# Products woven into two attention streams, early norms, pools handed over tile by tile, and a later quantised product in a twelve-stage Perceiver kernel

## The chip, the cores and the metric

The kernel runs on one core of a Trainium2 chip. A core has five engines that run side by side, each through its instructions in order: TensorE (PE in the profile, its weight loads PEld), VectorE (DVE), ScalarE (ACT), GpSimd (POOL) and SyncE (SP), which here only issues DMAs. The metric is the device time of the whole program in microseconds (us); the median of three runs stands for a kernel.

## The reference

x has 16 sequences of 64 tokens with 256 features; a context has 16 sequences of 1601 rows. Twelve blocks follow each other, and each adds to x what it computes from the layer norm of x:

```python
x = x + L0_xattn(norm(x), ctx)      # softmax attention over the context, 16 heads
x = x + L0_attn(norm(x))            # sqrt(D)*x + position, 4 layers of linear attention + relu MLP, last norm
x = x + L0_ffn(norm(x))             # 8 experts, capacity, gelu
x = x + L1_xattn(norm(x), ctx)      # slot attention: 3 iterations with a GRU
x = x + L1_attn(norm(x))            # softmax attention among 64 tokens, bias, own input
x = x + L1_ffn(norm(x))             # router, 8 experts, 2 integration steps, refinement
x = x + L2_xattn(norm(x), ctx, mask)# relu(scores)^2 attention over the context
x = x + L2_attn(norm(x))            # attention by relu features
x = x + L2_ffn(norm(x))             # 16 experts, 8 of them chosen, and a shared one
x = x + L3_xattn(norm(x), ctx)      # softmax attention over the context
x = x + L3_attn(norm(x))            # causal softmax attention, relative bias
h = norm(x)                         # L3_ffn: rows rounded to 8 bits
s = max(abs(h), axis=-1) / 127
x = x + (clip(round(h / s), -128, 127) @ Wq.T) * s * weight_scale + bias
```

Here norm subtracts the mean of a row and divides by its standard deviation.

## The kernel before, in words

The 1024 tokens are NT = 8 tiles of 128 rows; x stays in SBUF as [128, 8, 256]. A product over 256 features is KC = 2 matmuls, into which the operand goes transposed, so that a stage starts as: statistics of each tile on VectorE (bn_stats, bn_aggr), a square root on ScalarE (rstd, L125), the normalised rows xln on VectorE, transposes on TensorE (tr), evictions, first product.

Each block is a method that opens pools of its own: sb and sb2 (SBUF, one and two buffers) and ps (PSUM). The list STAGES calls them in order; the last two blocks share l3_attn. Weights come through one pool that lives for the whole program (w2 with eight buffers, w8 with three). A pool is released at the end of its stage, and its bytes go to the stage behind. By default a tile on bytes of released pools waits for every user of those pools.

The order on an engine is partly written. keep_in_program_order pins an instruction behind the one that was traced before it on its engine; what is not pinned is ordered by a scheduler when the program is built. self.mm and self.tr (L2196, L2202) pin TensorE's instructions while self.pinned is set, and the class Written (L50) pins whatever VectorE, ScalarE or GpSimd get through it; linear attention uses it for all three (V, A, G).

Stage by stage, where the change reaches:

- l0_xattn and l2_xattn run through stream (L2091). It walks over pairs of context chunks of 128 rows: 16 sequences of NCH = 13 chunks are 208 chunks and 104 turns, and 9 turns more ahead of them. In turn k it issues the scores of turn k + 1 (weights), the projections of keys and values 18 chunks ahead (project, PSUM tag "bk"), and the weighted sums of chunks 2k and 2k + 1 (values, tag "acc"); a sequence is finished four chunks after its end (finish, which divides by the sums and fills hT). The last nine turns have no projections. Behind the stream self.lin makes the output product of all eight tiles, and add_to_x (L345) adds each to x.
- l0_attn works on two halves of x, a and b, of four tiles each. A half has its own buffers (class Half). measure takes statistics of a pair of tiles, norm normalises a pair, turn transposes a pair and evicts it to hT. project, attend and feed are generators that yield after each step; go(it, n) lets one run n steps, and mix lets the attention of one half run with the MLP (feed) of the other. begin makes the two norms at the start (of x, then of sqrt(D) x + position). The squares of the context for a later stage are taken on ScalarE in between, from pieces that come over ScalarE's DMA queue.
- l3_attn calls token_attention, whose loop at L2354 has ten turns. Turn t makes the scores of tile t, the values of tile t - 1 and the output product of tile t - 2. An object then adds the quantised block: prepare (L1989) takes one or two finished tiles, norms them, finds the largest value, scales, rounds by adding a large number, clamps (L2011) and writes f_xq; turn (L2017) transposes f_xq into f_qT; product multiplies, adds and stores a tile. In each turn one ready tile gets turn and product.

## Time and profile before

| what | us |
|---|---|
| median of three runs (3853.12 to 3859.05) | 3857.69 |
| profiled execution | 3857.84 |
| its span, first to last instruction | 3856.1 |
| TensorE busy | 3540.6 |
| VectorE busy | 1996.7 |
| ScalarE busy | 1455.9 |
| GpSimd busy | 1258.6 |

The span's 40 slices show TensorE's busy share and its granted clock, in tenths:

```
PE   8999999987999899999987998999999789999985
PEclk9999999998999889999989999999999979999987
```

Where the stages lie on the span, by the first transposes or products of each: l0_xattn to 865, l0_attn to 1331, l0_ffn to 1477, l1_xattn to 1999, l1_attn to 2090, l1_ffn to 2416, l2_xattn to 3080, l2_attn to 3196, l2_ffn to 3559, l3_xattn to 3713, the last layer to the end at 3856.

How to read the profile's lines. A timeline line is: start, duration, engine, line of the source, operation, output<-inputs, shapes, type, count, and in brackets how long the engine stood ahead of it and whose result ended that. A waits line is: who waited for whom, total, times, longest. A line of the chain that ended last is: start, duration, what ran. Helpers record under their own line: L2203 is tr, L2198 is mm, L58 is Written, L191 is lin. The granted clock is TensorE's, as a share of its full rate.

### The profile page before, as it was taken

To read this page: it belongs to the slowest core of one execution; us is meant where nothing else is said; L and a number is where in the kernel's file an instruction comes from. 1 tells how busy PE (TensorE), PEld (TensorE's weight loads), DVE (VectorE), ACT (ScalarE), POOL (GpSimd) and SP (SyncE) were. 2 spreads that over 40 slices of the span, in tenths; PEclk is the share of its full clock that TensorE was granted. 3 is DMA by queue.
4 is the path that set the end of the run, shared out by engine and by line. 5 is a ranking of instruction groups with operands and counts; after the bars stand their busy time and mean duration, and the time that the engine had idled before them with its cause. 6 is when DMAs were issued, how large, how long until landed. Compare 5 with 4: busy or idle time off the path is not lost.

```text
span 3856.1 us, 71175 instructions
## 1 busy us (share of the span) xinstructions
PE 3540.6 (92%) x31178; PEld 2237.7 (58%) x31178; DVE 1996.7 (52%) x3673; ACT 1455.9 (38%) x2067; POOL 1258.6 (33%) x749
## 2 busy tenths in 40 slices
PE   8999999987999899999987998999999789999985
PEld 4555555553566555555545666676767555555554
DVE  4333333335555435556556644577767655333346
ACT  2333333333444302444423434366666612111222
POOL 1555555551110002334331100477777530000011
PEclk9999999998999889999989999999999979999987
DMA  3111110001333214422301000311111004111730
GB/s 123 37 37 37 37 37 34 22 26 53 93 98 94 77 30 170 142 84 95 107 26 38 1 6 1 108 37 55 37 55 37 11 1 170 39 39 29 297 149 13
DMA packets 99678, 248.86 MB, mean 65 GB/s; under 512 B 8180, under 2 KB 69247, under 8 KB 97192
## 3 DMA queue, kind: packets, MB, share of 16 engines
q1 hardware_dynamic: 92456, 217.05, 15.9%
q10 hardware_dynamic: 6912, 27.27, 2.3%
q8 instruction: 245, 4.01, 0.4%
q14 instruction: 65, 0.53, 0.0%
HBM read 243.24 MB, written 1.05 MB: 63 GB/s over the span
## 4 chain that ended last, share of the span: by engine, by line
PE 77%; DVE 12%; ACT 7%; issue 2%; DMA 1%; POOL 0%; ACTq 0%; SPq 0%; DVEq 0%; POOLq 0%
PE sc L2198 15%; PE pk L2198 15%; PE lin L2198 6%; PE acc L2198 6%; PE lin L191 5%; PE lin_t L2198 5%; ACT e L319 5%; PE pu L2198 3%; PE gate L1770 3%; PE up L1770 3%; PE pc L1397 3%; PE prz L2198 2%; PE lin_t L178 2%; PE gelu_t L1307 2%; PE turn L2203 2%
## 5 line engine op out<-in xcount | busy, mean ns | idle before, releaser
L2134 POOL TENSOR_TENSOR tot<-tot,e 128x1024 f32<-128x1024 f32 (+1 forms) x340 | 803.4, 2363 | 375.0 <-ACT e L319 252.0
L262 DVE TENSOR_REDUCE m<-sc 128x4 f32<-128x2048 f32 x96 | 220.1, 2293 | 273.3 <-PE sc L2198 272.2
L1537 DVE SCALAR_TENSOR_TENSOR e<-sc,row_L_xattn_nbias,free 128x2048 f32<-128x2048 f32 x104 | 244.3, 2349 | 124.4 <-PE sc L2198 118.8
L1539 ACT ACTIVATE e<-e 128x2048 f32<-128x2048 f32 x104 | 198.8, 1912 | 242.8 <-DVE e L1537 242.8
L319 ACT ACTIVATE e<-sc 128x2048 f32<-128x2048 f32 x104 | 195.3, 1877 | 241.4 <-PE sc L2198 233.8
L2198 PE MATMUL sc<-qb,kT 32*128 32x128 f32 x6656 | 247.0, 285 | 39.3 <-DVE m L276 12.3
L2198 PEld LDWEIGHTS sc<-qb,kT 32*128 32x128 f32 x6656 | 208.1, 188 | 84.6 <-issue 25.1
L2198 PE MATMUL acc<-e,v 128*32 128x128 f32 x6656 | 228.4, 278 | 6.8 <-ACT e L1540 6.8
L2198 PEld LDWEIGHTS acc<-e,v 128*32 128x32 f32 x6656 | 171.3, 110 | 105.6 <-issue 95.0
L2198 PE MATMUL pk<-cT,wk 128*128 128x512 f32 (+1 forms) x512 | 207.6, 534 | 3.6 <-DVE rows L292 3.6
L2198 PE MATMUL pk<-wv,cT 128*128 128x256 f32 x832 | 208.6, 392 | 0.0
L1540 ACT ACTIVATE e<-e 128x2048 f32<-128x2048 f32 x104 | 198.9, 1912 | 3.3
L2198 PE MATMUL pk<-cT,wkv 128*128 128x512 f32 (+1 forms) x512 | 196.3, 524 | 0.0
L2198 PE MATMUL pk<-wkv,cT 128*128 128x256 f32 x832 | 196.3, 386 | 0.0
L2198 PEld LDWEIGHTS pk<-wv,cT 128*128 128x128 f32 x832 | 149.1, 189 | 75.3 <-issue 57.2
L2198 PEld LDWEIGHTS pk<-wkv,cT 128*128 128x128 f32 x832 | 153.2, 190 | 28.5 <-issue 4.3
L1397 PE MATMUL pc<-ew,eh 128*128 128x256 f32 x640 | 156.7, 387 | 0.0
L1774 ACT ACTIVATE g<-gate 128x512 f32<-128x512 f32 x68 | 40.7, 599 | 293.2 <-PE gate L1770 293.2
L942 POOL TENSOR_TENSOR e<-e,mx 128x512 f32<-128x512 f32 x96 | 81.7, 883 | 212.7 <-DVE mx L941 212.7
L2198 PE MATMUL sc<-kT,qb 32*128 32x512 f32 (+2 forms) x1536 | 139.5, 462 | 12.2 <-ACT e L319 0.7
L2198 PE MATMUL pu<-cn,e 128*64 128x257 f32 (+1 forms) x1248 | 143.7, 387 | 5.6 <-POOL e L952 5.6
L2198 PE MATMUL sc<-cT,qT 128*64 128x512 f32 (+1 forms) x768 | 142.2, 519 | 0.9 <-DVE qT L900 0.5
(488 smaller groups left out, 6392.4 us busy)
## 6 DMA issues: line engine op xcount, KB each, us to landing
cT<-in_ctx_t SPq DMA_DIRECT2D x128, 832.0 KB
cn<-in_ctx_n SPq DMA_DIRECT2D x32, 1664.0 KB
piece<-in_ctx_n ACTq DMA_DIRECT2D x32, 640.0 KB
w<-in_L_attn_W SPq DMA_DIRECT2D x8, 1024.0 KB
piece<-in_ctx_n ACTq DMA_DIRECT2D x16, 384.0 KB
w<-in_L_ffn_W SPq DMA_DIRECT2D x16, 256.0 KB
down<-in_L_ffn_w_down SPq DMA_DIRECT2D x16, 256.0 KB
gate<-in_L_ffn_w_gate SPq DMA_DIRECT2D x16, 256.0 KB
```

Source lines behind the costliest of these rows:

```text
L178: nc.tensor.matmul(pm, w[:, k, n * P : (n + 1) * P], xT[:, k, h * 512 : (h + 1) * 512], start=(k == 0), stop=(k == kc - 1),)
L191: nc.tensor.matmul(pm, xT[:, k, t * P : (t + 1) * P], w[:, k, :], start=(k == 0), stop=(k == kc - 1))
L262: nc.vector.tensor_reduce(x.m4[:, g, :, i], pm, AX.X, ALU.max)
L319: nc.scalar.activation(e, pm, AF.Exp, scale=0.25)
L942: pin(nc.gpsimd.tensor_tensor(p.e, p.e, p.mx.unsqueeze(2).to_broadcast(p.shape), ALU.subtract))
L1397: nc.tensor.matmul(pc[:, n, j, :], s.eh[i][:, c, tok], ew2[:, c, cols], start=False, stop=(c == 3))
L1537: nc.vector.scalar_tensor_tensor(e16, pm16, nb, free[:, at : at + P].unsqueeze(1).to_broadcast([P, 16, P]), ALU.add, ALU.mult)
L1539: nc.scalar.activation(e, e, AF.Relu)
L1540: nc.scalar.activation(e, e, AF.Square)
L1770: nc.tensor.matmul(pm[-1], w[:, k, n * P : (n + 1) * P], xT[:, k, tok], start=(k == 0), stop=(k == KC - 1))
L2134: nc.gpsimd.tensor_tensor(tot[:w], x.first if c == 1 else tot[:w], e[:w], ALU.add)
L2198: ins = self.nc.tensor.matmul(*args, **kw)
```

## The change

- **Output products in the streams.** stream gets a function out(t), which makes the product of tile t and adds it to x, with a PSUM tile of the projections' tag. Turns k = 96 to 102 call it for tiles 0 to 6 behind the scores of the next turn and ahead of the sums; tile 7 comes after the last finish. The call of self.lin goes.
- **Linear attention's start.** begin becomes start(s, p) for one pair. For half a (both pairs) and b (first pair) statistics, start and norm are traced before the projection of a, with VectorE's part not pinned; ScalarE's part stays pinned. The second pair of b is traced between steps of project(a). GpSimd's addition of the last norm's bias to x is moved behind project(a). Half makes its tiles in a written order, PSUM of attention has a pool of its own (ps_kv), and small statistics tiles move from sb2 to sb.
- **Linear attention's loop.** In feed, measure(y, 1) is a step of its own behind the last product; the loop runs it with one more go(fd, 1), behind the first step of project.
- **Pools.** All stage pools get reuse_waits="tile": a tile waits only for users of earlier tiles on its own bytes (in PSUM, its own bank). The pools of l0_attn, l1_xattn, l1_ffn, l2_attn and l3_xattn get side="right", which lays them from the other end of SBUF.
- **Last layer.** The norm of prepare is one small VectorE instruction and two ScalarE activations per tile in place of one VectorE instruction; the clamp is on GpSimd for tiles 0 to 5. The loop takes tiles that were prepared two or more turns before, all at once; behind the loop turn and product alternate.

```diff
@@ -51,11 +51,13 @@
     def __init__(self, tc, engine):
-        self.tc, self.engine = tc, engine
+        self.tc, self.engine, self.pinned = tc, engine, True
...
         def issue(*args, **kw):
-            self.tc.keep_in_program_order(getattr(self.engine, name)(*args, **kw))
+            ins = getattr(self.engine, name)(*args, **kw)
+            if self.pinned:
+                self.tc.keep_in_program_order(ins)
         return issue
...
@@ -325,8 +327,13 @@
-            self.stream(ps, sb2, load, wk, wv, copy, weights, finish, extra)
-            self.lin(ps, wo, hT, self.add_to_x, tag="acc")
+            def out(t):
+                pm = ps.tile([P, D], F32, tag="bk", name="lin", padded_shape=[P, 512])
+                for k in range(KC):
+                    self.mm(pm, hT[:, k, t * P : (t + 1) * P], wo[:, k, :], start=(k == 0), stop=(k == KC - 1))
+                self.add_to_x(t, pm)
+
+            self.stream(ps, sb2, load, wk, wv, copy, weights, finish, out, extra)
...
@@ -422,20 +430,22 @@
                     s.x = self.x[:, i * HT : (i + 1) * HT, :]
-                    for name, shape in (
-                        ("y", [P, HT, D]), ("n", [P, HT, D]), ("tmp", [P, HT, D]), ("kz", [P, HT, D]),
-                        ("va", [P, HT, 2, 136]), ("hT", [P, KC, 512]), ("qT", [P, KC, 512]), ("h1T", [P, 8, 512]),
-                    ):
-                        setattr(s, name, sb.tile(shape, F32, tag=f"{name}{i}", name=name))
+
+                shapes = dict(y=[P, HT, D], n=[P, HT, D], tmp=[P, HT, D], kz=[P, HT, D], va=[P, HT, 2, 136],
+                              hT=[P, KC, 512], qT=[P, KC, 512], h1T=[P, 8, 512])
+
+                def make(s, *names):
+                    for name in names:
+                        setattr(s, name, sb.tile(s.shapes[name], F32, tag=f"{name}{s.i}", name=name))
...
-                mv = sb2.tile([P, 2, 2], F32, tag=f"ln_mv{s.i}", name="ln_mv")
+                mv = sb.tile([P, 2, 2], F32, tag=f"ln_mv{s.i}", name="ln_mv", bufs=2)
                 for j in range(2):
-                    st = sb2.tile([P, 6], F32, tag="ln_st", name="ln_st", bufs=3)
+                    st = sb.tile([P, 6], F32, tag="ln_st", name="ln_st", bufs=3)
                     V.bn_stats(st, src[:, 2 * p + j, :])
                     V.bn_aggr(mv[:, j, :], st)
-                r = sb2.tile([P, 2], F32, tag=f"ln_r{s.i}", name="ln_r")
+                r = sb.tile([P, 2], F32, tag=f"ln_r{s.i}", name="ln_r", bufs=2)
                 V.tensor_scalar(r, mv[:, :, 1], 1.0, 1e-5, ALU.mult, ALU.add)
@@ -549,7 +559,7 @@
-                    pk = ps.tile([P, 2, 512], F32, tag="kv", name="pk")
+                    pk = ps_kv.tile([P, 2, 512], F32, tag="kv", name="pk")
                     for g in range(2):
@@ -620,11 +630,13 @@
                     V.tensor_tensor(s.y[:, t, :], pm, s.y[:, t, :], ALU.add)
-                    if t % 2:
-                        measure(s, s.y, t // 2)
-                    elif t:
+                    if t == 1:
+                        measure(s, s.y, 0)
+                    elif t == 2:
                         finish(s, 0, last)
                     yield
+                measure(s, s.y, 1)
+                yield
                 finish(s, 1, last)
@@ -640,27 +652,17 @@
-            def begin(s):
-
-                measure(s, s.x, 0)
-                yield
-                measure(s, s.x, 1)
-                yield
-                for p in range(2):
-                    mv, r = s.by[p]
-                    less = sb2.tile([P, 2], F32, tag=f"less{s.i}", name="less")
-                    V.tensor_scalar(less, mv[:, :, 0], -1.0, 0.0, ALU.mult, ALU.add)
-                    V.reciprocal(r, r)
-                    V.tensor_scalar(r, r, math.sqrt(D), 0.0, ALU.mult, ALU.add)
-                    for j in range(2):
-                        t = 2 * p + j
-                        A.activation(s.n[:, t, :], s.x[:, t, :], AF.Identity, bias=less[:, j : j + 1])
-                        V.scalar_tensor_tensor(s.y[:, t, :], s.n[:, t, :], r[:, j : j + 1], pos, ALU.mult, ALU.add)
-                    measure(s, s.y, p)
-                    yield
-                    norm(s, s.y, p)
-                    yield
-                G.tensor_tensor(s.x, s.x, lnf[:, D:].unsqueeze(1).to_broadcast([P, HT, D]), ALU.add)
+            def start(s, p):
+
+                mv, r = s.by[p]
+                less = sb.tile([P, 2], F32, tag=f"less{s.i}", name="less", bufs=2)
+                V.tensor_scalar(less, mv[:, :, 0], -1.0, 0.0, ALU.mult, ALU.add)
+                V.reciprocal(r, r)
+                V.tensor_scalar(r, r, math.sqrt(D), 0.0, ALU.mult, ALU.add)
+                for j in range(2):
+                    t = 2 * p + j
+                    A.activation(s.n[:, t, :], s.x[:, t, :], AF.Identity, bias=less[:, j : j + 1])
+                    V.scalar_tensor_tensor(s.y[:, t, :], s.n[:, t, :], r[:, j : j + 1], pos, ALU.mult, ALU.add)
@@ -668,22 +670,42 @@
-            less = sb.tile([P, 1], F32, tag="less", name="less")
+            less = sb.tile([P, 1], F32, tag="minus", name="minus")
             nc.gpsimd.memset(less, -1.0)
...
             a, b = Half(0), Half(1)
+
+            a.make("h1T")
+            b.make("h1T", "tmp")
+            a.make("tmp", "hT", "kz", "va", "qT")
+            b.make("n", "kz", "va", "hT", "qT", "y")
+            a.make("y", "n")
             w = weights(0)
+
+            V.pinned = False
+            for s, n in ((a, 2), (b, 1)):
+                for p in range(n):
+                    measure(s, s.x, p)
+            for s, n in ((a, 2), (b, 1)):
+                for p in range(n):
+                    start(s, p)
+                    measure(s, s.y, p)
+                for p in range(n):
+                    norm(s, s.y, p)
+            V.pinned = True
             for s in (a, b):
                 nc.gpsimd.memset(s.va[:, :, :, 128:136], 1.0)
-            st = begin(a)
-            go(st, 4)
-            pr, st2 = project(a, w), begin(b)
+            pr = project(a, w)
+            go(pr, 3)
+            measure(b, b.x, 1)
             go(pr, 1)
-            go(st)
-            for n in (1, 1, 1, 2, 1, 99):
-                go(pr, n)
-                go(st2, 1)
-            go(st2)
+            start(b, 1)
+            measure(b, b.y, 1)
+            go(pr, 1)
+            norm(b, b.y, 1)
+            go(pr)
+            for s in (a, b):
+                G.tensor_tensor(s.x, s.x, lnf[:, D:].unsqueeze(1).to_broadcast([P, HT, D]), ALU.add)
             at, pr = attend(a, w), project(b, w)
@@ -699,6 +721,7 @@
                     go(pr, 1)
+                    go(fd, 1)
                     go(fd2, 1)
...
@@ -775,9 +798,9 @@
         with ExitStack() as ctx:
-            sb = ctx.enter_context(tc.tile_pool(name="l1x", bufs=1))
-            sb2 = ctx.enter_context(tc.tile_pool(name="l1x2", bufs=2))
-            ps = ctx.enter_context(tc.tile_pool(name="l1x_ps", bufs=1, space=PSUM))
+            sb = ctx.enter_context(tc.tile_pool(name="l1x", bufs=1, side="right", reuse_waits="tile"))
+            sb2 = ctx.enter_context(tc.tile_pool(name="l1x2", bufs=2, side="right", reuse_waits="tile"))
+            ps = ctx.enter_context(tc.tile_pool(name="l1x_ps", bufs=1, space=PSUM, reuse_waits="tile"))
             wq = self.w2(d["L1_xattn_Wq"], "wq")
...
@@ -1543,16 +1566,21 @@
-            self.stream(ps, sb2, load, wkv[:, :, :D], wkv[:, :, D:], copy, weights, finish)
-            self.lin(ps, wo, hT, self.add_to_x, tag="acc")
+            def out(t):
+                pm = ps.tile([P, D], F32, tag="bk", name="lin", padded_shape=[P, 512])
+                for k in range(KC):
+                    self.mm(pm, hT[:, k, t * P : (t + 1) * P], wo[:, k, :], start=(k == 0), stop=(k == KC - 1))
+                self.add_to_x(t, pm)
+
+            self.stream(ps, sb2, load, wkv[:, :, :D], wkv[:, :, D:], copy, weights, finish, out)
...
         with ExitStack() as ctx:
-            sb = ctx.enter_context(tc.tile_pool(name="l2a", bufs=1))
-            sb2 = ctx.enter_context(tc.tile_pool(name="l2a2", bufs=2))
-            ps = ctx.enter_context(tc.tile_pool(name="l2a_ps", bufs=1, space=PSUM))
+            sb = ctx.enter_context(tc.tile_pool(name="l2a", bufs=1, side="right", reuse_waits="tile"))
+            sb2 = ctx.enter_context(tc.tile_pool(name="l2a2", bufs=2, side="right", reuse_waits="tile"))
+            ps = ctx.enter_context(tc.tile_pool(name="l2a_ps", bufs=1, space=PSUM, reuse_waits="tile"))
             w = self.w8(d["L2_attn_Wqkv"], "wqkv")
...
@@ -1996,9 +2024,11 @@
                 xln = sb2.tile([P, 2, D], F32, tag="f_x", name="f_x")
+                minus = sb2.tile([P, 2], F32, tag="f_m", name="f_m")
+                nc.vector.tensor_scalar(minus[:, :n], mv[:, :n, 0], -1.0, 0.0, ALU.mult, ALU.add)
                 for j, t in enumerate(us):
-                    nc.vector.tensor_scalar(
-                        xln[:, j, :], self.x[:, t, :], mv[:, j, 0:1], r[:, j : j + 1], ALU.subtract, ALU.mult)
+                    nc.scalar.activation(xln[:, j, :], self.x[:, t, :], AF.Identity, bias=minus[:, j : j + 1])
+                    nc.scalar.activation(xln[:, j, :], xln[:, j, :], AF.Identity, scale=r[:, j : j + 1])
                 am = sb2.tile([P, 2], F32, tag="f_am", name="f_am")
@@ -2008,7 +2038,8 @@
                     nc.vector.tensor_scalar(q, xln[:, j, :], rx[:, j : j + 1], big, ALU.mult, ALU.add)
-                    nc.vector.tensor_scalar(q, q, big + 127.0, big - 128.0, ALU.min, ALU.max)
+                    clamp = nc.gpsimd if t < NT - 2 else nc.vector
+                    clamp.tensor_scalar(q, q, big + 127.0, big - 128.0, ALU.min, ALU.max)
                     xq[t] = sb2.tile([P, D], BF16, tag="f_xq", name="f_xq", bufs=4)
@@ -2088,7 +2119,8 @@
-    def stream(self, ps, sb2, load, wk, wv, copy, weights, finish, extra=None):
+    def stream(self, ps, sb2, load, wk, wv, copy, weights, finish, out, extra=None):
+
@@ -2168,6 +2200,8 @@
                 es[k + 1] = weights([(xs[n // NCH], n % NCH) for n in (2 * k + 2, 2 * k + 3)])
+            if N // 2 - NT <= k < N // 2 - 1:
+                out(k - N // 2 + NT)
             jobs = sorted(plan.get(k, []), key=lambda job: job[1])
@@ -2189,6 +2223,7 @@
         finish(xs[B - 1])
+        out(NT - 1)
         self.pinned = False
@@ -2365,23 +2400,22 @@
                 next(rest, None)
-            now = ready[:1]
+            now = [u for u, since in ready if t > since + 1]
             for u in now:
...
                 then.product(u)
-                ready.remove(u)
+            ready = ready[len(now) :]
             if t > 1:
...
                     then.prepare(us)
-                    ready += us
-        for u in ready:
+                    ready += [(u, t) for u in us]
+        for u, _ in ready:
             then.turn(u)
-        for u in ready:
             then.product(u)
```

All other stage pools change like those of l1_xattn, with or without side="right" as said.

## The prediction

> **What bounds the kernel now.** I read the page's first part, then the waits of TensorE, then TensorE's timeline at each stage's seam, and last what releases the wait there.
>
> ```profile
> PE 3540.6 (92%) x31178; PEld 2237.7 (58%) x31178; DVE 1996.7 (52%) x3673; ACT 1455.9 (38%) x2067; POOL 1258.6 (33%) x749
> ...
> PE 77%; DVE 12%; ACT 7%; issue 2%; DMA 1%; POOL 0%; ACTq 0%; SPq 0%; DVEq 0%; POOLq 0%
> ```
>
> TensorE is the bound: 3540.6 of a span of 3856.1 us. The change removes no matmul, so it can win only from the 315 us in which TensorE stands, and from matmuls that run at half clock after it stood. The waits of TensorE say where it stands:
>
> ```profile
> PE trb L2203 <- ACT f_xq L2013: 28.9, 5, 8.9
> PE tr L157 <- DVE xln L145: 24.5, 7, 7.4
> PE lin L2198 <- DVE hT L58: 18.7, 8, 9.8
> PE lin_t L2198 <- DVE hT L58: 12.8, 9, 5.4
> PE tr L2203 <- DVE n L58: 10.9, 3, 7.5
> ...
> PE tr L2203 <- DVE xln L2261: 10.3, 1, 10.3
> ```
>
> The columns are total, count and longest. Nearly all are the first transposes of a stage waiting for a layer norm (xln, n), or the last layer waiting for its quantised rows (f_xq). TensorE's timeline shows the seams one by one:
>
> ```profile
> 872.38 1.13 PE L2203 MATMUL tr<-cst,n 128*128 128x128 f32 x4 [7.53 <-DVE n L58]
> 874.15 5.58 PE L2198 MATMUL lin<-wkv,hT 128*128 128x512 f32 x8 [0.64 <-DVE hT L58]
> ...
> 884.34 5.40 PE L2198 MATMUL lin_t<-hT,wq 128*128 128x512 f32 x8 [4.17 <-DVE hT L58]
> ...
> 904.63 5.69 PE L2198 MATMUL lin<-wkv,hT 128*128 128x512 f32 x8 [9.81 <-DVE hT L58]
> ...
> 1030.98 3.70 PE L2198 MATMUL lin<-wkv,hT 128*128 128x512 f32 x8 [1.37 <-DVE hT L58]
> ...
> 1334.60 2.17 PE L157 MATMUL tr<-cst,xln 128*128 128x128 f32 x8 [7.42 <-DVE xln L145]
> ```
>
> Is the norm late for its data or for its buffers? At the seam before 1334.60 the first half's rows of x are final at 1296.6, yet VectorE's first statistics of the new stage start at 1331.62, right behind the last write of x for the other half: eight tiles at once, with VectorE idle for stretches in between. Other engines show the same:
>
> ```profile
> POOL raw L812 <- DVE x L723: 183.7, 1, 183.7
> ...
> POOL less L1982 <- PE pa L2198: 138.8, 1, 138.8
> ```
>
> One stage's first instruction stood until the last user of the stage before. So the pool, not the data, is what ends these waits.
>
> **The change, part by part.** Gains in us on TensorE's path.
>
> A, first stream to linear attention. Now: last exp ends 854.8, four rounds of sums end 857.2, 28 matmuls of products (1.13 + 5.45) with a wait of 1.10, x final 865.3, then table load 1.28 and a norm chain to 872.38; up to 904.63 TensorE stands 7.53 + 0.64 + 4.17 + 0.94 + 9.81 = 23.1. Changed: seven of eight products (4 matmuls, 0.86 each at full clock) go into cycles k = 96 to 102. A cycle is 3.44 long; TensorE has 1.04 free in the earlier ones of these and 0.2 to 0.4 in the last ones, where its sums are added, so four products lie beside other work and three cost about 0.5: 1.5 later. Their hT is ready (a sequence finishes four chunks after its end), their bank is that of the projections, which have ended. Their additions on VectorE (0.42 each) and the seven statistics (0.6) lie in VectorE's idle time. The square roots stay behind the last exp, now 856.3; queued behind them on ScalarE are the identities of n. Table load, root and 4 us of chain give the first n at about 862.5, the product of tile 7 ends near 862.6, so the transposes start about 863 instead of 872.4. The second pair follows some 3.5 later while TensorE computes 4.7; b's first pair leaves about 2. The projection of b starts about 887 instead of 904.6: **17** (8 to 20). GpSimd's addition to x (2.64 and 2.34) is moved behind the projection; the addition to y that it was ahead of gets earlier.
>
> B, linear attention's loop. The two statistics (1.45) are put behind the eviction of hT. Six waits of 1.37 as at 1030.98: at most 8.2; some 0.3 each remains: **6.5** (3 to 7).
>
> C, to the first experts: only tiles 6 and 7 wait for the last x at 1331.6. Statistics, norm, transposes, copies and router of two tiles take 6, so the router is complete near 1338 instead of 1346.2; the router's own chain (7.27 idle) stays: **7** (5 to 8.5).
>
> D, to slots. cT is issued at 1477.5 and lands 10.73 later in the chain; behind it three waits near 2.0 and one of 2.56, with VectorE at raw and bias. Earlier issue and earlier GpSimd and VectorE work: 1510 becomes about 1502: **7.5** (-2 to 10; where these tiles lie on the last expert's bytes, SP's loads stay late).
>
> E to J, the same step at seams without a product: 10.32 + 2.31 at 2006.5 gives **9.5** (7 to 11.5); 6.60 at 2095.4 **5** (3 to 7); 5.97 at 2421.7 **4.5** (3 to 7); the second stream's end (3.66, and products that hold the last sums up by 1.5) **4.5** (-7 to 7); 1.46 + 2.37 + 0.78 into the 17 experts **3** (1 to 6); 5.49 at 3564.5 **4** (2 to 5.5). In each about 1 to 1.5 stays for the tiles that are final last.
>
> K, into the last layer:
>
> ```profile
> 3710.23 4.53 DMA row_L_attn_b_attn<-in_rows
> ...
> 3714.78 4.87 DMA hot<-in_buckets
> ...
> 3719.79 6.99 PE pb L1955 x122
> ```
>
> The loads, SP's first of this stage, are issued when the stage before ends; issued earlier they free the 3.26 and 1.94 before pb, not the seven of pb: **5** (2 to 7).
>
> L, last layer. A pair of turns takes 3795.60 to 3817.35, 21.75, of which TensorE stands 8.93 for f_xq. The chain from the projection (end 3807.4) to f_xq is 10. Changed: the norm's two VectorE instructions (1.78 for both beside GpSimd) become four on ScalarE (0.45 each by the row of f_xq, 0.91 for two: 1.8), behind an exp with its table load (3812.4 to 3815.0), up to 2.4 later; the clamp goes from 0.49 for two on VectorE to GpSimd. The trace has no clamp there; the nearest row is its 128x256 TENSOR_SCALAR of linear attention, 1.09, so 2.2 for two (by the 128x2048 one, 5.37, it would be 0.7 each and 1.4; I take the row of the same width). The chain is 12 to 14, but the product comes one whole turn later (values 4, projection 1, scores 1.1: 6 more cover). Waits near 4 stay, and the softmax chain from scores to exp, 7.7, becomes the next bound of a turn. A pair goes from 21.75 to about 19.5, three times: **6.5** (-3 to 10; without the later turn it would be the loss).
>
> Sum: 17 + 6.5 + 7 + 7.5 + 9.5 + 5 + 4.5 + 4.5 + 3 + 4 + 5 + 6.5 = **80**.
>
> **The clock.** The eight matmuls lin<-wkv,hT take 5.58 and 5.69 after the waits of 7.53 and 9.81, and 3.70 after one of 1.37: 1.9 more. The granted clock is 0.5 there and behind every wait over 3.5 us. The Trainium skill, "TensorE: Matmul & The Clock Gate", Part 1 on the clock gate, says that the ramp may be left out of a model, as under 1% of a span; then the sum is 80. By the row, some nine seams lose a wait above 3.5 us, at 1 to 1.9 each, two or three of them in A: **13** (0 to 25). I take the row, for there are many ramps here, not one. 80 + 13 = 93; the profiled execution is 3857.84 (span 3856.1 and 1.74 around it), which is the median to 0.15: **3765**.
>
> **A rule against it.** "ScalarE: Activation LUTs", What ACT_TABLE_LOAD costs: a switch of function set is 1283 ns and a drain of about 1380, 2.66. Early norms put square roots between the exps of the running stage, each with a switch there and back. The trace:
>
> ```profile
> 867.15 1.28 ACT L58 ACT_TABLE_LOAD   x1 [12.36 <-DVE ln_st L58]
> 868.45 0.30 ACT L58 ACTIVATE ln_r<-ln_r 128x2 f32<-128x2 f32 x2
> ...
> 3812.19 0.20 ACT L131 ACTIVATE f_r<-f_r 128x2 f32<-128x2 f32 x1 [2.06 <-DVE f_r L130]
> 3812.41 1.28 ACT L2321 ACT_TABLE_LOAD   x1
> ```
>
> Load follows root, and root follows load, within 0.02: 1.3, no drain. In the second stream ScalarE has 0.94 free in a cycle of 4.76: a switch both ways is 2.6 and costs 1.7 a cycle by the row, 4.4 by the page; in four cycles 7 or 18. I take 7 as the low end there, and none in the sum, for the roots can also stand behind the stream.
>
> **Rivals.** Half of it (chance 0.18): the next stage's tiles lie on bytes of the last users after all, or the last tile's chain takes the wait over. VectorE's eight norms need 4 us and each seam keeps 4 to 5 of its idle time; A keeps 10, D and K nothing: 45, **3812**. For it: xln and raw are large tiles; against it: x's first half is final 35 us early at C.
>
> More of it (0.13): early transposes fill the waits wholly and no ramp is left: 106 + 12, **3740**. Against it: the last tile of a seam has nothing to hide behind.
>
> No effect (0.03): the norms are ordered last on VectorE as now, **3857**. Against it: the gaps in VectorE's timeline.
>
> Slower (0.04): the table switches. Nine seams with eight tiles are 72 roots; with a switch both ways on ScalarE's path each costs 2.6. It decides at 93 / 2.6 = 36 of them on the path; with 42, **3873**. Against it: TensorE, not ScalarE, sets the pace at most seams.
>
> **Numbers.** The main case has 0.62, its own range 3745 to 3790. A measurement tells about 0.2%, 7.7 us, from no change. The main case, more and half are all faster: 0.93. No effect is mostly same: 0.03; slower 0.04. The range 3735 to 3815 leaves out the far half of the half case, the ends of the main one and what is above.
>
> **What would show it.** Right: at the seams of C, E, F, G and J the waits of tr for xln under 2; statistics of the next stage ahead of the last x; lin<-wkv,hT near 887; the six waits of 1.37 under 0.5; raw and less no longer among GpSimd's longest waits; f_xq waits near 4 each, with f_x on ScalarE. Wrong: the same waits with another releaser, many more ACT_TABLE_LOAD than now in 1477 to 2416, sums of the streams waiting for e, or f_xq waits over 8.

## The result, and the profile after

The changed kernel takes **3824.39 us** (median of 4 runs, 3822.40 to 3827.85) where the kernel before takes 3855.40 on the same chip (4 runs, 3846.85 to 3859.05): the ratio is 0.9924, with a 95% interval of 0.9904 to 0.9943. That is 31 us less by the medians and 0.76% less by the ratio. The forecast was 3765, with a range of 3735 to 3815: the sign was right, the gain a third of the 93 us forecast, and the time lies outside the range.

The first part of the page and the shares of the chain that ended last, after the change:

```profile
span 3821.0 us, 71159 instructions
PE 3522.3 (92%) x31163; PEld 2225.8 (58%) x31178; DVE 1991.1 (52%) x3664; ACT 1457.4 (38%) x2080; POOL 1260.9 (33%) x755
...
PE 77%; DVE 12%; ACT 8%; issue 2%; POOL 1%; DMA 0%; ACTq 0%; DVEq 0%; SPq 0%; POOLq 0%
```

The span fell by 35.1, TensorE's busy time by 18.3 and its standing time from 315.5 to 298.7, by 16.8 alone. No matmul was taken out; the 18.3 go with the granted clock, whose mean went from 0.959 to 0.964. DMA fell from 1% of the chain to nothing. TensorE's waits after the change (total, count, longest):

```profile
PE tr L159 <- DVE xln L147: 23.6, 8, 7.2
PE trb L2238 <- ACT f_xq L2044: 15.4, 4, 7.7
...
PE lin_t L2233 <- DVE hT L58: 10.7, 9, 5.4
...
PE lin L2233 <- DVE hT L58: 10.7, 8, 7.4
PE tr L2238 <- DVE n L58: 10.4, 4, 5.7
...
PE tr L2238 <- DVE xln L2296: 8.8, 1, 8.8
```

The wait for f_xq halved (28.9 to 15.4) and that for hT fell from 18.7 to 10.7. But the waits for a first norm, which eight of the twelve steps of the forecast lived on, are nearly all there: 24.5 became 23.6, 10.9 became 10.4, 10.3 became 8.8. GpSimd's wait at raw, 183.7 before, is gone from its longest waits, so the buffers did come free earlier (less still waits, 122.2 for a sc); what was to follow from it did not.

To see which step paid, the two traces are cut at the same instructions of TensorE. In us, by their start times:

| Step | Stretch, up to | Before | After | Gain | Forecast |
|---|---|---|---|---|---|
| A | first po (linear attention) | 914.98 | 910.54 | 4.4 | 17 |
| B | its last h1T product | 411.83 | 404.92 | 6.9 | 6.5 |
| C | pc of the experts' count | 26.41 | 25.92 | 0.5 | 7 |
| D | first pu of the slots | 156.99 | 149.66 | 7.3 | 7.5 |
| – | last pn of the slots | 485.61 | 484.54 | 1.1 | 0 |
| E | first lin_t of the 64-token attention | 14.94 | 13.50 | 1.4 | 9.5 |
| F | last po of the feed-forward | 404.56 | 407.97 | -3.4 | 5 |
| G | first sc of the second stream | 46.19 | 46.26 | -0.1 | 4.5 |
| H | first lin of the 64-feature attention | 624.04 | 622.41 | 1.6 | 4.5 |
| I | last down product of the experts | 473.05 | 470.85 | 2.2 | 3 |
| J | first lin_t behind them | 8.48 | 8.25 | 0.2 | 4 |
| K | first sc of the last attention | 179.18 | 174.01 | 5.2 | 5 |
| L | the last matmul | 105.09 | 98.03 | 7.1 | 6.5 |

B, D, K and L give 26.5, forecast 25.5. The eight seams A, C, E to J give 6.8, forecast 54.5.

Two things have to be read beside this table. First, a stretch gets shorter by less waiting or by a higher clock. TensorE's standing time fell by 7.1 in B and 8.4 in L, but only by 1.7 in D and 2.3 in K; the rest of D and K is busy time (147.9 to 142.2 in D, 162.1 to 159.2 in K, at granted clocks of 0.90 and 0.93, then 0.92 and 0.94). Second, each column is one trace, and a stretch with the same order does not always take the same time. In the kernels below that have the changed kernel's pools, and its order in the stretch, A ends at 910.4 to 914.3, B takes 404.9 to 407.1, D 149.6 to 154.1, F 404.7 to 410.7, H 622.4 to 624.7, I 463.6 to 473.1, K 173.5 to 175.5 and L 96.2 to 101.4; C, E and J stay within 0.7. So the sizes at A and D are known to some 4 us only, and F, H and I are not told from nothing. The same holds for the clock: the forecast's 13 stands against the 18.3 above, and how much of that the change brought stays open.

TensorE's timeline of the changed kernel at the first three failed seams, A, C and E (in brackets the idle time ahead and what ended it):

```profile
858.82 1.13 PE L2233 MATMUL lin<-wo,xT 128*128 128x256 f32 x4 [2.85 <-DVE xT L2092]
865.66 0.48 PE L2238 MATMUL tr<-cst,n 128*128 128x128 f32 x1 [5.71 <-DVE n L58]
...
875.75 5.99 PE L2233 MATMUL lin<-wkv,hT 128*128 128x512 f32 x8 [7.36 <-DVE hT L58]
884.32 3.70 PE L2233 MATMUL lin_t<-hT,wq 128*128 128x512 f32 x8 [2.14 <-DVE hT L58]
894.55 3.41 PE L2233 MATMUL lin<-wkv,hT 128*128 128x512 f32 x4 [4.82 <-ACT qT L58]
...
900.51 5.37 PE L2233 MATMUL lin<-wkv,hT 128*128 128x512 f32 x8 [2.11 <-DVE hT L58]
...
1317.64 0.94 PE L159 MATMUL tr<-cst,xln 128*128 128x128 f32 x4 [1.80 <-DVE xln L147]
1323.18 1.22 PE L159 MATMUL tr<-cst,xln 128*128 128x128 f32 x4 [4.61 <-DVE xln L147]
...
1984.75 1.97 PE L2238 MATMUL tr<-cst,xln 128*128 128x128 f32 x8 [8.79 <-DVE xln L2296]
```

At A the waits 7.53 + 0.64 + 4.17 + 0.94 + 9.81 = 23.1 of before have become 2.85 + 5.71 + 1.36 + 7.36 + 2.14 + 4.82 + 2.11 = 26.4 (the 2.85 lies ahead of the last product, where the kernel before waited 1.10): the products are out of the way, and what was won is waited for again. At C one wait of 7.42 is two, of 1.80 and 4.61. At E 10.32 became 8.79.

Why is the norm still late? VectorE's timeline at C in the changed kernel:

```profile
1305.58 0.42 DVE L58 TENSOR_TENSOR y<-lin,y 128x256 f32<-128x256 f32 x1 [2.77 <-PE lin L2233]
1308.97 0.42 DVE L58 TENSOR_TENSOR y<-lin,y 128x256 f32<-128x256 f32 x1 [2.96 <-PE lin L2233]
...
1312.42 0.42 DVE L58 TENSOR_TENSOR y<-lin,y 128x256 f32<-128x256 f32 x1 [1.75 <-PE lin L2233]
...
1312.95 0.74 DVE L58 TENSOR_SCALAR n<-y,ln_mv,ln_r 128x256 f32<-128x256 f32 x2
1313.61 0.42 DVE L143 BATCH_NORM_STATS2 ln_st<-x 128x6 f32<-128x256 f32 x1
```

The first statistics (L143) start at 1313.61. Their rows of x were final at 1285.15, when a's last addition ended. The bytes that they write were last used at 1139.5; this is read from the tiles' addresses in the built program and the last user of the same bytes in the trace. Between 1285.15 and 1313.61 VectorE stood idle for 21.4 us, in pieces such as the 2.77, 2.96 and 1.75 above. Neither the pool nor the data held them. They stand, in the order in which the built program holds VectorE's instructions, behind b's additions to y, and VectorE takes its instructions in that order. The same view at E: rows of x long final, bytes free at 1942.5, first statistics at 1978.58, idle between 20.5. At A and G the bytes are free long before too, and from when the first tile's rows are final to the first statistics VectorE stands idle for 18.4 and 15.5.

The other seams are different. At F, H, I and K the first tile's rows are final early (2028.6, 3017.7, 3129.9 and 3596.0), but the bytes of the statistics, read in the same way, are in use until late: the last matmul that takes them as operands ends at 2055.4, 3054.9, 3146.0 and 3688.1, and from there VectorE is idle for 5.6, 0.6, 3.9 and 2.2 before the first statistics. At J the rows themselves are late (2.6).

So at A, C, E and G there were two causes one behind the other, and the change took away only the first; at F, H, I and K the bytes still hold for most of the time, since the last users of the stage before lie on them. Three theories went to the chip: **order** (where the next stage's first instructions stand in VectorE's queue), **pools** (the hand-over still holds something, or brings more than the stretches show), and **data** (the last rows of x, and the chain behind them, set the stretch whatever is ahead).

### The profile page after: what moved, and what is told of

Read it like the earlier page. It is cut to its first block, busy times and chain, and to the rows that moved or that the text cites. A ratio compares the mean times of both kernels' runs of the same rounds, so it can differ in the third digit from the quotient of the medians.

```text
span 3821.0 us, 71159 instructions
## 1 busy us (share of the span) xinstructions
PE 3522.3 (92%) x31163; PEld 2225.8 (58%) x31178; DVE 1991.1 (52%) x3664; ACT 1457.4 (38%) x2080; POOL 1260.9 (33%) x755
## 3 DMA queue, kind: packets, MB, share of 16 engines
HBM read 243.24 MB, written 1.05 MB: 64 GB/s over the span
## 4 chain that ended last, share of the span: by engine, by line
PE 77%; DVE 12%; ACT 8%; issue 2%; POOL 1%; DMA 0%; ACTq 0%; DVEq 0%; SPq 0%; POOLq 0%
PE sc L2233 15%; PE pk L2233 14%; PE lin L2233 7%; PE acc L2233 6%; PE lin_t L2233 5%; PE lin L193 5%; ACT e L321 4%; PE pu L2233 4%; PE gate L1798 3%; PE up L1798 3%; PE pc L1420 3%; PE prz L2233 2%; PE lin_t L180 2%; PE gelu_t L1330 2%; PE turn L2238 2%
## 5 line engine op out<-in xcount | busy, mean ns | idle before, releaser
L1560 DVE SCALAR_TENSOR_TENSOR e<-sc,row_L_xattn_nbias,free 128x2048 f32<-128x2048 f32 x104 | 244.3, 2349 | 122.2 <-PE sc L2233 118.3
L2233 PEld LDWEIGHTS sc<-qb,kT 32*128 32x128 f32 x6656 | 206.1, 187 | 80.6 <-issue 24.5
L1803 DVE TENSOR_TENSOR hT<-up,g 128x512 f32<-128x512 f32 x68 | 47.0, 692 | 178.7 <-PE up L1798 174.6
```

The source lines that it names most:

```text
L1560: nc.vector.scalar_tensor_tensor(e16, pm16, nb, free[:, at : at + P].unsqueeze(1).to_broadcast([P, 16, P]), ALU.add, ALU.mult)
L2233: ins = self.nc.tensor.matmul(*args, **kw)
```

## The experiments

Each stretch below is measured between the same instructions as in the table; a single time without a range is that of one run. The kernel before took 3850.5 to 3857.0 beside them, so a few us between totals say little.

**What the pools are worth, from both sides.** First the kernel before with nothing but the pools of the change:

```
-            sb = ctx.enter_context(tc.tile_pool(name="l1x", bufs=1))
+            sb = ctx.enter_context(tc.tile_pool(name="l1x", bufs=1, side="right", reuse_waits="tile"))
...
```

> The kernel before with the pools alone changed: handed over tile by tile, alternate stages from the other end, own PSUM pool for kv; nothing else. Theory (order): freed bytes do not move a norm that stands behind the running stage in VectorE's queue, so the seams that wait for xln keep their waits within 2 us each (7.42, 10.32, 6.60, 5.97, 5.49 of before) and only the seams that waited for a first load or for GpSimd gain: slots 7, last layer 5, in all 12 to 16 faster than before, about 3840. Rival (pools): the handover is the greater part of the 31 that the whole change gives, 25 or more, about 3830.

Measured: 3843.05 (3836.05 to 3848.30) against 3857.04, ratio 0.9961 (0.9948 to 0.9975), 14 us faster. Then the changed kernel with the pools' waits back:

```
-            sb = ctx.enter_context(tc.tile_pool(name="l1x", bufs=1, side="right", reuse_waits="tile"))
+            sb = ctx.enter_context(tc.tile_pool(name="l1x", bufs=1, side="right"))
...
```

> The changed kernel with every pool handed over whole again, the ends of SBUF kept. Theory (order): it loses what the handover gave at slots and at the last layer, 12 to 16, about 3838, and the seams that wait for xln stay within 2 us of the changed kernel. Rival (pools): it loses 25 or more, about 3850.

Measured: 3843.19 (3838.66 to 3843.81), ratio 0.9962 (0.9949 to 0.9976): 19 more than the changed kernel. So the pools give 14 to 19 of the 31, where the forecast's steps that lean on them (C to K; H has the products too) had 50. The 19 lie between what order (12 to 16) and pools (25 or more) expected. The stretches say where. Step D is 152.3 with the pools alone, 158.6 with the pools' waits back and 149.7 with the change. Of the 4.7 that the first has less than the kernel before 1.7 are waits, and of the 8.9 that the second has more than the change 5.8; the rest is TensorE's busy time. TensorE's timeline of the second of these kernels shows waits there that the changed kernel does not have:

```profile
1474.94 1.08 PE L2233 MATMUL sc<-cT,qT 128*64 128x512 f32 x4 [1.43 <-DMA cT<-in_ctx_t]
1478.55 7.53 PE L2233 MATMUL sc<-cT,qT 128*64 128x512 f32 x26 [2.53 <-DMA cT<-in_ctx_t]
```

They are for a load of the stage. Step K goes the same way: 178.5 with the waits back against 174.0 and 174.3 with the pools, 2.1 to 2.2 of it in waits. Where SP's loads or GpSimd's own instructions opened a stage, the hand-over by tile let them go; at C (25.2 with the waits back, 25.9 with the change) it gave nothing, and at G about 1 (a wait of 5.86 with the waits back, 4.97 with the change).

**The products inside the stream.** The changed kernel with the output products of both streams behind the last cycle again:

```
-            if N // 2 - NT <= k < N // 2 - 1:
-                out(k - N // 2 + NT)
...
-        out(NT - 1)
+        for t in range(NT):
+            out(t)
```

> The changed kernel with all eight output products behind the last turn of both streams. Theory (order): in the first stream the statistics stand behind the last finish with or without early products, so the products in the turns are worth their own 6 to 8 us there at most and 1 to 2 in the second: 4 to 8 slower than the changed kernel, about 3830. Rival: the early products are what the norms need, and without them the start of linear attention is where it was before and later still: 15 to 20 slower, about 3842.

Measured: 3827.63 (3824.91 to 3831.55), 3 more than with the change, with ranges that overlap. So neither theory's figure came: order had 4 to 8. The first po starts at 912.4 instead of 910.5. With the products behind, the matmuls of the products end at 862.6 instead of 859.9, and the wait for the first n falls from 5.71 to 4.34: 1.4 of the 2.6 is given straight back, because the norm's chain doesn't start earlier.

**The order at C and E.** Statistics, root and norms of the first four tiles of two stages are written by hand into the stage before: at C into the last feed-forward of linear attention, at E into the slots' last update but one, ahead of its pn.

```
+            e = self.norm_early(early, V, A, x)     # 4 tiles: statistics, root
+            go(fd, 2)
+            self.xln0 = self.norm_early_end(V, e, x)   # reciprocal, 4 norms
...
-            self.transpose(ps, xln, xT)
+            self.transpose(ps, self.xln0, xT[:, :, : T // 2])
+            self.transpose(ps, xln, xT[:, :, T // 2 :])
```

> The changed kernel with the norms of the first four tiles of two stages written by hand into the running stage: those of the experts inside linear attention's last MLP, those of the 64-token attention inside the last slot update, in tiles of a pool of their own. Theory (order): with the order moved and bytes and data as they were, the wait of 8.79 ahead of the transposes at the 64-token attention falls under 2 and the 2.36 behind it under 1, 8 to 10 gained there; at the experts 1.80 and 4.61 fall to about 2 together, 4 gained; in all 11 to 14 faster than the changed kernel, about 3811. Rival (chain): the norms of the last tiles, not their place in the queue, set these waits; nothing changes beyond 2 us at either.

Measured: 3817.91 (3816.50 to 3821.37), ratio 0.9898 (0.9883 to 0.9914). TensorE at E:

```profile
1955.10 7.39 PE L2275 MATMUL sc<-cT,qT 128*64 128x512 f32 x32 [2.67 <-DVE qT L956]
...
1983.31 1.03 PE L2275 MATMUL pn<-mvg,uT 128*128 128x256 f32 x4
1984.17 1.04 PE L2280 MATMUL tr<-cst,early_x 128*128 128x128 f32 x8
1987.80 4.94 PE L2275 MATMUL lin_t<-xT,wqkv 128*128 128x512 f32 x7 [2.59 <-DVE xT L123]
```

The wait of 8.79 is gone: the transposes follow pn at once, and the stretch E falls from 13.50 to 3.84. At C the stretch falls from 25.92 to 22.78. What was changed is where these norms stand, and that they write to a pool of their own; since the bytes had been free long before, order was the cause here. But 5.3 came back ahead of E: the inserted norms made VectorE's qT late, the scores waited 2.67 for it and then took 7.39 instead of 5.81, at a granted clock of 0.78 instead of 1.00, and the stretch of the slots went from 484.5 to 489.9. In all the kernel is 6.5 below the change, where order expected 11 to 14. In its trace B and D are 2.2 and 4.2 longer besides; so they are in the kernel of G below (407.1 and 154.0), whose edit lies behind both.

So the next kernel has E alone, with the inserted work split: statistics ahead of that update's sums, root ahead of its pn, norms ahead of the sums of the last update.

```
+                update(sa, None, sb_ if n else None, None if an else (first_part, root_part))
...
+                update(sb_, an and an[0], None, None if an else (last_part, lambda: None))
```

> The changed kernel with the norms of the first four tiles ahead of the 64-token attention written by hand in three places of the last two slot updates where VectorE is idle: statistics ahead of the first one's sums, root with the slots' root, norm ahead of the last one's sums. Theory (order, and the price of the place): the wait of 8.79 goes as with the norms in one place, and the wait of 2.67 ahead of the scores that they cost there, and the slow clock behind it, do not come: 8 to 10 gained at this seam against the changed kernel, where e4 gained 4.3. Rival: the gain was given back by the table loads or by VectorE's load, not by the place; then no more than 5.

Measured: 3818.57. Stretch E 3.83, the slots 484.55: the same 9.7 without the price. The next stretch up to the feed-forward's first hotT gives 2.6 back (113.67 to 116.25); it is no price of the step, for with the same norms in the combined kernel below that stretch takes 112.72.

**The order at A.** The change issues the first chains of a and of b's first pair in one block, ahead of a's projection. Here b's first pair is moved behind a's first products, one instruction group at a time:

```
-            for s, n in ((a, 2), (b, 1)):
-                for p in range(n):
-                    start(s, p)
...
-            go(pr, 3)
+            go(pr, 1)
+            start(b, 0)
+            measure(b, b.y, 0)
+            go(pr, 1)
+            norm(b, b.y, 0)
+            go(pr, 1)
```

> The changed kernel with one move in the start of linear attention: the first pair of half b (start, statistics, norm) is written behind the first transposes and evictions of half a instead of ahead of them. Theory (order in the queue): the wait of 7.36 ahead of the first key and value product is the eviction of hT standing behind b's chain on VectorE; it falls to about 1, and the projection of b starts 4 to 6 earlier. Rival (chain or GpSimd): the 7.36 is a's own chain, or the 2.96 that one VectorE instruction takes beside GpSimd's additions; then it stays above 4.

TensorE in this kernel:

```profile
873.68 5.91 PE L2237 MATMUL lin<-wkv,hT 128*128 128x512 f32 x8 [1.05 <-DVE hT L58]
...
884.16 5.40 PE L2237 MATMUL lin_t<-hT,wq 128*128 128x512 f32 x8 [4.13 <-DVE hT L58]
...
894.40 2.99 PE L2237 MATMUL lin<-wkv,hT 128*128 128x512 f32 x4 [3.12 <-ACT qT L58]
...
899.93 3.67 PE L2237 MATMUL lin<-wkv,hT 128*128 128x512 f32 x8 [1.69 <-DVE hT L58]
```

The four waits 7.36 + 2.14 + 4.82 + 2.11 = 16.4 are 1.05 + 4.13 + 3.12 + 1.69 = 10.0, and from the stream's last product to the first po 50.97 becomes 44.71, 6.3 less (5.6 less from the stream's last sums, 55.2 to 49.6). The whole kernel took 3810.39; 6.9 of its 14.0 come from another place, where nothing was changed (see the last section).

On top of it, a's first norms and b's first statistics go into the stream's last cycles, between the products:

```
+            if early and k >= N // 2 - NT:
+                early(k - N // 2 + NT)     # statistics at 2, 4, 6; roots and first norms at 7, 8
```

> As e5, and the statistics of tiles 0 to 5 and the norms of half a written by hand into the first stream's last turns: a pair's statistics two products later, the roots behind the last exp, the norm of the first pair ahead of the last finish, that of the second behind it. Theory (order): VectorE's idle time of 12 to 18 that these statistics had and did not use is used; the first transposes start about 860 on the changed kernel's scale instead of 865.7, the waits ahead of them (2.85, 5.71, 1.36, 7.36 in the changed kernel) fall from 17 to about 8, and the projection of b starts 9 to 12 earlier than in the changed kernel. Rival (chain): the last product and the table load set the start; less than 3 beyond e5.

Measured: 3820.21; the stretch is 42.59, 2.1 below the one before and 8.4 below the change. The wait of 5.71 for the first n is gone, but the stream's last product now waits 4.51 instead of 2.85, and hT 4.14 and 4.50. The longer wait of that product lies ahead of where the stretch begins: from the stream's last sums it is 49.2 us, against 49.6 in the kernel before this one, so only 0.5 of the 2.1 was won. That is what the rival had (less than 3), and short of order's 9 to 12. What the limit is then, VectorE's chain from the last finish or the last product, no run separates.

The third thing at A is GpSimd. In the change its additions to y and x lie beside VectorE's start of the norms; here the two additions to x go behind the first layer.

```
-            for s in (a, b):
-                G.tensor_tensor(s.x, s.x, lnf[:, D:].unsqueeze(1).to_broadcast([P, HT, D]), ALU.add)
             at, pr = attend(a, w), project(b, w)
...
+            for s in (a, b):
+                G.tensor_tensor(s.x, s.x, lnf[:, D:].unsqueeze(1).to_broadcast([P, HT, D]), ALU.add)
             for l in range(1, 4):
```

> The changed kernel with linear attention's two additions of the last bias to x on GpSimd (2.5 us each) moved behind its first layer, so that they no longer lie beside the chains of a's and b's first norms. Contention theory: VectorE's scalar_tensor_tensor of 2.96 and 3.07 us fall back to about 0.88, and the waits for hT and qT (7.36 and 4.82) shorten by 2 to 4 us together: first stream's end to first po product 47 to 49 us (51.0 with the change), median 3820 to 3823. Order theory: the chain waits for its place in the queue and for ScalarE's tables, not for GpSimd; single instructions get shorter but the stretch stays within 1 of 51.0, median within 2 of 3824.

VectorE and GpSimd in the changed kernel:

```profile
865.52 0.88 DVE L58 SCALAR_TENSOR_TENSOR y<-n,ln_r,cst 128x256 f32<-128x256 f32 x2
868.85 2.96 DVE L58 SCALAR_TENSOR_TENSOR y<-n,ln_r,cst 128x256 f32<-128x256 f32 x2
887.33 3.07 DVE L58 SCALAR_TENSOR_TENSOR y<-n,ln_r,cst 128x256 f32<-128x256 f32 x2 [2.72 <-ACT n L58]
...
869.02 2.51 POOL L58 TENSOR_TENSOR y<-y,row_L_attn_bk.0_7235 128x1024 f32<-128x1024 f32 x1 [11.50 <-DVE n L58]
...
887.77 2.35 POOL L58 TENSOR_TENSOR x<-x,row_L_attn_lnf_s 128x1024 f32<-128x1024 f32 x1 [13.76 <-ACT n L58]
```

And with the additions later:

```profile
871.40 2.96 DVE L58 SCALAR_TENSOR_TENSOR y<-n,ln_r,cst 128x256 f32<-128x256 f32 x2
889.47 0.88 DVE L58 SCALAR_TENSOR_TENSOR y<-n,ln_r,cst 128x256 f32<-128x256 f32 x2 [2.72 <-ACT n L58]
```

The instruction of 3.07 is back at 0.88; the first, 2.96, stays, since the addition to y still lies beside it. The wait for qT falls from 4.82 to 0.93, the stretch from 50.97 to 47.90, 3.1 less (2.4 from the last sums), in the middle of what contention expected; the time, 3818.69, is a little below it.

**One step that was right, B.** The statistics of the second pair go back to one loop step later:

```
-                    if t == 1:
-                        measure(s, s.y, 0)
-                    elif t == 2:
-                        finish(s, 0, last)
+                    if t % 2:
+                        measure(s, s.y, t // 2)
+                    elif t:
+                        finish(s, 0, last)
...
```

> The changed kernel with one part undone: linear attention's statistics of the second pair go back to one loop step later, in the feed-forward's order of before. Prediction's step (a gain of 6.5 from six waits of about 1.37 us on TensorE): first po product to the loop's end 411 to 413 us (404.9 with the change), the six waits of 1.3 to 1.4 back, median 3830 to 3833. Rival, the loop's gain came from the pools or the kept tiles: stretch within 2 of 404.9, median within 3 of 3824.

Measured: 3829.92; the loop takes 412.01 instead of 404.92 and the six waits of 1.37 are back. 7.1, all of step B.

**The last layer, L, in its two parts.** The norm and the clamp back on VectorE, the later turn kept:

```
-                    nc.scalar.activation(xln[:, j, :], self.x[:, t, :], AF.Identity, bias=minus[:, j : j + 1])
-                    nc.scalar.activation(xln[:, j, :], xln[:, j, :], AF.Identity, scale=r[:, j : j + 1])
+                    nc.vector.tensor_scalar(
+                        xln[:, j, :], self.x[:, t, :], mv[:, j, 0:1], r[:, j : j + 1], ALU.subtract, ALU.mult)
...
-                    clamp = nc.gpsimd if t < NT - 2 else nc.vector
+                    clamp = nc.vector
```

> The changed kernel with the last layer's quantising norm and clamp on VectorE as before, and the products still two turns later. Theory: the later turn gave the gain of 7 in the last layer, and the norm on ScalarE costs or gives less than 2; from the layer's first scores to the end within 2 of the changed kernel, and the longest wait for f_xq falls from 7.70 to about 5 since the chain is shorter. Rival: relieving VectorE gave the gain; then 4 to 7 slower.

Measured: 3829.95, stretch 99.49 (98.03 with the change), waits for f_xq 15.8. And the old turn order with the new norm:

```
-            now = [u for u, since in ready if t > since + 1]
+            now = [u for u, since in ready][:1]
...
```

> The changed kernel with only the last layer's later turn undone: tiles are turned and multiplied in the order of before, while ScalarE's norm and GpSimd's clamp stay. By the trace of the changed kernel the stretch from the last attention's first scores to the end takes 98.0 us, with 15.4 us of waits on f_xq in 4 places (105.1 and 28.9 in 5 places before the change). Turn theory (as the prediction has it: the norm moved to other engines is a loss of about 3 without the later turn): 107 to 110 us, waits on f_xq of 31 or more, median near 3834. Rival, norm theory: the norm's move gives most of it, stretch 99 to 102, waits 16 to 21, median near 3827.

Measured: 3819.88, stretch 104.72. The waits, last layer of this kernel:

```profile
PE trb L2238 <- ACT f_xq L2044: 30.3, 5, 10.1
```

105.09 before, 104.72 with the new norm alone, 99.49 with the later turn alone, 98.03 with both: the turn gives 5.6 to 6.7, the norm's engines 0.4 to 1.5. The same last layer as in the change took from 96.2 to 101.4 in the other kernels here, so the first is a gain of a size that stays open by some 3, and the second is not told from nothing. The expected loss of 3 did not come. The whole time of this kernel is below that of the change all the same, mostly because the 64-feature attention, unchanged in it, took 107.31 instead of 114.38: here the stretch has to be read, not the total.

**Does it add up?** b behind a's products, the norms at C, and the split norms at E together:

> The changed kernel with three orders written by hand together: linear attention's b half behind a's products, the expert stage's first four norms inside the last feed-forward of linear attention, the 64-token attention's first four norms split over the slots' last updates. Order theory, the sum of the stretches measured one at a time: 6.3 + 3.1 + 7.1 = 16.5 less, 3805 to 3811 median, ratio to the kernel before 0.987 to 0.989. Rival (what is won at one place is given back at a later one by the clock granted or by another wait): at most 8 less, 3816 or more.

Measured: 3810.97 (4 runs, 3798.96 to 3814.65), ratio 0.9877 (0.9857 to 0.9897), 13 less than the change. The three stretches are 44.72, 22.78 and 3.84, each what it was alone. The total is at the slow edge of what was expected; in the profiled run the 64-feature attention took 117.25 and the last layer 99.74.

**A seam where the data are late, G.** Statistics and root of the first four tiles stand before the last update of the feed-forward; the norms alone are behind the last addition to x:

```
             refine(a)
+            self.l2_first = self.first_statistics(early, self.x[:, : NT // 2, :])
             update(b, 1)
             refine(b)
```

> The changed kernel with one order written by hand at the seam into the second stream: statistics, root and reciprocal of the first four tiles stand on VectorE ahead of the last update of the feed-forward before (their rows of x are final at 2381.2, VectorE then stands idle for 15.5 us until the first statistics at 2399.05), and the four norms alone follow the last addition to x. Order theory: the first norm is ready after 0.4 instead of 2.9 us, the wait of tr for xln of 4.97 falls to 2.3 to 2.8, and the stretch from the feed-forward's last po to the stream's first sc goes from 46.2 to 43.5 to 44.2. Rival, the last rows of x are what the stretch waits for: the first wait falls, a later one grows by as much, stretch 45.5 to 46.5.

TensorE with the change, and then in this kernel:

```profile
2402.40 2.08 PE L159 MATMUL tr<-cst,xln 128*128 128x128 f32 x8 [4.97 <-DVE xln L147]
```

```profile
2397.66 7.07 PE L1483 MATMUL po<-fw,fT 128*128 128x256 f32 x32
2406.81 1.52 PE L173 MATMUL tr<-cst,xln 128*128 128x128 f32 x8 [2.08 <-DVE xln L58]
2410.76 1.99 PE L173 MATMUL tr<-cst,xln 128*128 128x128 f32 x8 [2.43 <-DVE xln L161]
```

The wait of 4.97 falls to 2.08, as order said; but the second half, whose rows of x are final last, now makes TensorE wait 2.43 (0.80 + 0.34 before). The stretch goes from 46.26 to 44.72: 1.5, between the two theories, where it takes 45.9 to 47.4 in the other kernels. Both seem to be at work here. The time was 3828.20. All four together:

> The kernel with the three orders by hand together and this fourth one. Order theory: 2.3 less than the three (3810.97 median, lowest 3798.96), so 3805 to 3810. Rival: within 1 of the three, where the last rows of x set the stretch; in both cases a spread of 5 or more, since the clock granted in the 64-feature attention differs from run to run.

Measured: **3808.66** (4 runs, 3805.01 to 3813.32), ratio 0.9875 (0.9858 to 0.9891): 16 less than the change and the lowest median, though the three together are within its spread. Its stretch G is 44.0, but B and D are 2.2 and 4.2 longer in its trace than in that of the three, so its total says nothing of G. Four orders written by hand bring 16 of the 59 us between the forecast and the change.

## Why the prediction was wrong

**The step that failed** is the last sentence of its first part: "So the pool, not the data, is what ends these waits." The evidence for it was sound as far as it went (x final early, VectorE idle, statistics right behind the last instruction of the stage before), and it excluded the data. It did not exclude a third cause that shows the same picture: the place in VectorE's own queue. The profile of before could not tell the two apart, since with the pool's wait in front the order behind it cannot be seen; GpSimd's raw and less, shown in support, were cases of another engine, whose queue had nothing else in it. Taken to the seams, this one inference carried C, E, F, G, H, I and J and most of A: 54.5 forecast, 6.8 measured. In its place the runs show the queue as the cause at C and E (3.1 and 9.7) and in part at A and G; at F, H, I and K the bytes were still in use, so that giving them back tile by tile freed them late. And even with the order mended the seams don't shrink to the 1 to 1.5 each that the forecast left for the last tiles: C and G keep waits of 2.74 and 2.43 for their second halves.

- **A, 17 forecast, 4.4 measured.** The products went into the turns as forecast, but the first n came at 865.66 and not at 863: the statistics stand behind the last finish. Then the change's own written order put b's first pair ahead of a's hT: 6.3 by its own run. The forecast of "887 for b's projection" (900.5 measured) had b's pair arriving beside TensorE's work, for free. GpSimd's additions were reckoned to be moved out of the way; they moved beside VectorE's chain and cost 2.4 to 3.1. These single corrections are not a sum: the norms in the stream on top of the first gave 0.5.
- **C, 7 forecast, 0.5; E, 9.5 forecast, 1.4.** Order, shown by hand-written order: 3.1 at C, 9.7 at E. With it E is worth what was forecast; C about half of it, as the second half's norms (waits of 2.74 and 0.61) and the router's chain stay.
- **F to J, 21 forecast, 0.5.** Only G was tried, and it is mixed: 1.5. In F the wait of 6.60 is now 5.41, and waits of 2.60 and 2.07 follow. At F, H and I the bytes come free late and at J the rows do; what order would give there no run shows.
- **B, D, K and L, 25.5 forecast, 26.5.** B by its own run, 7.1. L: the sum was right, the split was not (a loss without the later turn was forecast, 0.4 gain measured). D and K are DMA and GpSimd at the head of a stage, which do wait for a pool; 4.7 to 8.9 and 4.5 to 4.9 by the two pool runs. But the sizes were hit by luck: of D's 7.3 and K's 5.2 only 1.7 and 2.3 are waits, and of the three waits near 2.0 that D was to lose, two of 2.02 are still there.
- **The clock, 13 forecast.** It was counted for waits that would go, and most of them stayed. TensorE's busy time fell by 18.3 all the same; with the spread between kernels of the same order it can't be tied to the change.
- **The rivals.** "Half of it" gave 3812 from bytes shared with the last users. The size was nearer, and at F, H, I and K its mechanism is what the addresses show; at A, C, E and G, where most was forecast, it was wrong, for the bytes were free. "The norms are ordered last on VectorE as now" had 0.03, named under no effect, and was dismissed because of "the gaps in VectorE's timeline". That is the wrong way round: an engine that stands idle with ready work behind the instruction at its head is just what a fixed order looks like. The table switches did not happen: 121 table loads after, 124 before.

## What to carry to other kernels

When a next stage starts late, name three candidates before costing it: its data, its bytes, and its place in the engine's queue; an idle engine in front of ready work speaks for the third. Look at which bytes the new tiles lie on, and who used them last. A change to the buffers alone wins only where the first instruction of the stage is a DMA or sits on an engine with an empty queue. Write work that fills another stage's gaps by hand, and split it over the gaps: in one piece it made the running stage 5.3 late, in pieces nothing. Compare the same stretch between the same instructions, not totals, when an effect is a few us.

## What the runs showed of the hardware

**The granted clock differs with one and the same order.** The 64-feature attention, which none of the experiments at A, B, C, E, G and L touch, took from 107.3 to 117.3 us, at granted clocks from 0.87 down to 0.76. The windows over it in the changed kernel and in the one with b behind (length, busy time and count of PE, PEld, DVE, ACT and POOL, granted clock, DMA share, GB/s), first the one, then the other:

```profile
3065.70:3180.10 114.40, 92.47 (x1081) 64.36 (x1081) 70.98 (x141) 19.24 (x26) 33.41 (x11) 0.78 0.06 22
```

```profile
3060.60:3168.10 107.50, 84.91 (x1082) 58.90 (x1081) 70.60 (x141) 19.23 (x26) 33.39 (x11) 0.85 0.07 24
```

The same work, and 21.9 and 22.6 us of idle time on TensorE, but a clock of 0.78 against 0.85, and 7 us. The Trainium skill, "TensorE: Matmul & The Clock Gate", Part 1, calls the window that decides the clock free-running, and its ramps different from run to run. The traces fit that, and put a size to it: 10 us of 3820 between the ends, as much as most steps here. They are of kernels that differ ahead of this stage, though; for runs of one kernel only whole times are there, and those of the three orders together went from 3798.96 at a mean clock of 0.966 to 3814.65 at 0.962.

**GpSimd and VectorE.** A scalar_tensor_tensor pair takes 0.88 alone and 2.96 to 3.07 beside a GpSimd addition of 2.35 to 2.52. "SBUF — State Buffer", section "SBUF: two separate sides", says that a VectorE instruction with two inputs in SBUF and a GpSimd one that reads SBUF take turns, each blocked for the whole of the other; 0.88 + 2.5 is 3.4, and the trace has a little less. At E something nearby shows which I had not expected, beside a memset, which reads nothing (VectorE, then GpSimd):

```profile
1980.81 2.15 DVE L132 TENSOR_SCALAR ln_r<-ln_mv 128x4 f32<-128x4 f32 x1
```

```profile
1979.33 3.52 POOL L2272 MEMSET vm<- 128x4096 f32 x1
```

An instruction on four values, 0.17 elsewhere, ends at 1982.96, with the memset's end at 1982.85. It lies in the chain of the wait of 8.79. The last layer has the same with and without the memset. In the kernel before (VectorE, then GpSimd):

```profile
3710.64 3.25 DVE L1979 CAST identb<-cst 128x128 bf16<-128x128 f32 x1
```

```profile
3710.30 3.51 POOL L2237 MEMSET vm<- 128x4096 f32 x1
```

With the pools handed over by tile the memset runs 10.7 us ahead of this cast, which then takes 0.22; with the pools' waits back it is beside it again, and takes 3.25. So part of what K won may be this stall; no run tells the two apart.
